# One product with B per unit, later stores of y, and results of the side work taken one step later over three banks

## The chip, the cores and the metric

The kernel runs on one core of one Trainium2 chip. The metric is the device time of one execution in microseconds; the median of several runs is given. The engines are named as the profile names them: PE is TensorE's matmul, PEld its weight load, DVE is VectorE, ACT is ScalarE, POOL is GpSimd, SP is SyncE, which issues the DMAs here.

## The reference

The input `x` is 16 images of 256 channels on 32 x 32 positions (1024 tokens). Two layers are added to it in turn, each on a group-normalised input:

```python
x = x + _L0_conv_ref(_gn(x), ...)   # layer norm, attention of 4 heads, feed-forward of 128
x = x + _L1_conv_ref(_gn(x), ...)   # state-space scan with 512 channels and 64 states
```

The second layer, cut to what matters here:

```python
u, z = jnp.split(xs @ in_proj_w.T, 2, axis=-1)
u = jax.nn.silu(causal_conv(u, conv_w, 4 taps) + conv_b)
dt, Bm, Cm = jnp.split(u @ x_proj_w.T, [DT_RANK, DT_RANK + D_STATE], axis=-1)
delta = jax.nn.softplus(dt @ dt_proj_w.T + dt_proj_b)
def step(h, inp):                       # over 1024 tokens
    d_t, B_t, C_t, u_t = inp
    h = jnp.exp(d_t[..., None] * A) * h + (d_t * u_t)[..., None] * B_t[:, None, :]
    return (h, jnp.einsum('bdn,bn->bd', h, C_t))
y = (ys + u * D) * jax.nn.silu(z)
return (y @ out_proj_w.T) * ctx         # ctx: sigmoid of a convolution over tokens
```

## The kernel before

**The scan.** Its work is cut into 4096 units, 256 for each of the 16 batches: two halves `t` of 512 tokens, four blocks `k` of 128 channels, four quarters `q`, eight units `i`. A unit holds four channels with all their 64 states: 128 partitions are 64 states times two channels, and `e` runs over the two other ones. The main loop (L973) emits for unit n, in this order:

- `load(n + 6)`: SP fetches delta times u for four channels, broadcast over the states, into a tile `dub` of 128 x 2 x 512 (seven buffers). One such load is 512 KB. At the start of a quarter it also fetches `pieces`, at the start of a half the tiles `bt` and `ct`.
- `inputs(n + 4)`: POOL multiplies `dub` in place by `bt` (the B of the reference), in two instructions of 128 x 512 (L869).
- `scan(n, 0)` and `scan(n, 1)`: DVE's scan over 512 tokens (L891). It reads the decays `a` from PSUM and the product from SBUF, and writes `h`.
- `decay(n + 2)`: PE picks the deltas of four channels out of `pieces` into two PSUM banks (L878) and ACT takes the exponential in place (L881). Pool `aps` has four banks, two units' worth; the banks of unit n + 2 are those that unit n's scans have read.
- steps of the side work, as many as are due (below).
- `outputs`: a generator that runs one stretch per unit for each finished quarter. PE multiplies `h` with the spread C (`cd`, L928) in two rounds, ACT copies each round to `y2` (L936), PE turns it (L940), ACT copies the result to `yo` (L948), and one unit later SP stores it in four DMAs (L954). The tile `yb`, one PSUM bank, is taken and half cleared on DVE at the start of each half `t` (L918). `cd`, 128 x 4096, is taken and cleared on POOL once in each batch (L903); `spread_c` fills it with eight activations (L907) in unit 6 of each half.

**The side work** is all that the next batch needs (`first_norm`, `attention_layer`, `scan_inputs`) and what the last one still lacks (`gate_and_store`), written as generators. Each `yield` gives the share of time that the step before it is held to be worth. The loop hands steps out by credit:

```python
if at >= (1 if b + 1 < B else 8):
    due += rate
    while due > 0.0:
        due -= next(side, 1e9)
```

Here `at` is the number of the unit in its batch, and `rate` is the sum of all shares divided by 247, so about one step is emitted in each unit; a small share lets two steps into one unit, a large one leaves a unit without a step. In the last batch only `gate_and_store` is left.

**Order.** The loop at the end (L1022 to L1032) ties each instruction of PE, ACT, DVE and POOL to the one before it on its engine, so every engine runs its instructions in the order in which they were written.

**PSUM.** Eight banks: four for the decays (`aps`), one for `yb`, one (`accp`) for the sums `av` of the attention, two (`mm`) for the side work's results. `psum()` takes its bank from `mm` while the scan runs, and from `mm` and `aps` in turn before and after it.

**Names that are spoken of later.** `group_norm`: mean (PE), subtraction (DVE L249), squares (ACT), variance (PE), reciprocal root (ACT L260, L261), product (DVE L264); it runs twice for a batch. `layer_norm`: the same by halves of 512 tokens (means L272, subtraction L279, reciprocal root L296 and L298, product L303); also twice. In `scan_inputs`, z is PE L607, tanh on ACT L612, product on DVE L596 in `finish_z`; `project` and `tap` are the causal convolution (L628, L633, L634, L642); softplus is `begin` (PE L713, ACT L715, L716), `more` (ACT L721, L722), `rest` (DVE L726, L727) and the logarithm (ACT L739). In `gate_and_store`, `us` and `ys` are joined on DVE (L787, L791), and the last product goes through `m_ps` (PE L816, DVE L803 and L805 in `finish`). L642, L682, L787, L791, L330, L584, L539 and L515 are the DVE instructions that read two tensors in SBUF.

Of the kernel before, what the change touches and what calls it, by code (L numbers as in the profile page):

```python
# [11 lines left out]
F32 = mybir.dt.float32  # L12
BF16 = mybir.dt.bfloat16
AF = mybir.ActivationFunctionType
ALU = mybir.AluOpType
# [4 lines left out]
P = 128  # L20
# [3 lines left out]
HL = 512  # L24
# [9 lines left out]
TB = 512  # L34
# [18 lines left out]
def attention_then_scan_kernel(  # L53
# [18 lines left out]
    nc = tc.nc  # L72
# [13 lines left out]
    hst = pool("hst", 1)  # L86
# [11 lines left out]
    def psum(name, dims=P):  # L98
        src = mm if beside["scan"] else next(alone)
        return src.tile([P, HL], F32, name=name, tag="mm" if src is mm else "a")[:dims]  # L100

    def work(name, n=L):
        return wide.tile([P, L + 2 + CONV], F32, name=name, tag="wide")[:, :n]
# [4 lines left out]
    def hs(h):  # L108
        return ts(h, HL)
# [73 lines left out]
    for k in range(KC):  # L183
# [5 lines left out]
        nc.sync.dma_start(rel[ts(k, P), :], t)  # L189


    def weights(*specs):
# [34 lines left out]
    def group_norm(src, dst):  # L227
# [33 lines left out]
        nc.scalar.activation(v, v, AF.Exp, scale=-0.5)  # L261
        yield 1.5
        for k in range(KC):
# [4 lines left out]
    def layer_norm(src, dst, g, b):  # L268
        def mean_of(parts, name):
            m = psum(name)  # L270
            for k in range(KC):
                nc.tensor.matmul(m, avg, parts[k], start=(k == 0), stop=(k == KC - 1))  # L272
            return m

        def centre(h, m):
            qs = []
            for k in range(KC):
                d = dst[k][:, hs(h)]
                nc.vector.tensor_tensor(d, src[k][:, hs(h)], m, ALU.subtract)  # L279
                q = hwork("ln_sq")  # L280
                nc.scalar.activation(q, d, AF.Square)
                qs.append(q)
            return qs

        m = mean_of([t[:, hs(0)] for t in src], "ln_m")
        yield 1
        q0 = centre(0, m)
        m = mean_of([t[:, hs(1)] for t in src], "ln_m")
        yield 1.2
        q1 = centre(1, m)  # L290
        vs = [mean_of(q0, "ln_v")]
        yield 1.2
        vs.append(mean_of(q1, "ln_v"))
        yield 1
        for v in vs:
            nc.scalar.activation(v, v, AF.Ln, bias=eps)  # L296
        for v in vs:
            nc.scalar.activation(v, v, AF.Exp, scale=-0.5)  # L298
        yield 2
        for h in range(2):  # L300
            for k in range(KC):
                d = dst[k][:, hs(h)]
                nc.vector.tensor_tensor(d, d, vs[h], ALU.mult)  # L303
                nc.scalar.activation(d, d, AF.Identity, bias=col(b, k), scale=col(g, k))
            yield 1.2
# [258 lines left out]
    def scan_inputs(b):  # L564
# [27 lines left out]
        ready = []  # L592

        def finish_z():
            for d, hf, z, t, ps in ready:
                nc.vector.scalar_tensor_tensor(z[:, hs(hf)], t, 1.0, ps, ALU.add, ALU.mult)  # L596
                if hf == 1:
                    nc.sync.dma_start(zs[ts(d, P), :], z)
            ready.clear()

        for d in range(ND):
            z = work("z")
            for hf in range(2):
                finish_z()
                ps = psum("z_ps")
                for k in range(KC):
# [124 lines left out]
        for d in range(ND):  # L731
            items = [more(d, *items[0]), begin(d, 1)]
            yield 1
            items[1] = more(d, *items[1])
            rest(*items[0])
            yield 1.4
            rest(*items[1])
# [32 lines left out]
    def gate_and_store(b):  # L770
# [39 lines left out]
        for o in range(KC):  # L810
            for hf in range(2):
                ps = psum("m_ps")
                for q in range(2):
                    first = o * HL + hf * 2 + q
                    for d in range(ND):
# [3 lines left out]
                        )  # L819
                    if q == 0:  # L820
                        finish()
# [43 lines left out]
    def inputs(n):  # L865
        b, t = units[n][:2]
        for e in range(2):
            v = loaded[n][:, e, :]
            nc.gpsimd.tensor_tensor(v, v, blocks[b, t]["bt"], ALU.mult)  # L869

# [28 lines left out]

    def spread_c(b, t):  # L900
        if t == 0:
            now["cd"] = hst.tile([P, TB // 16, P], F32, name="cd", tag="cd")
            nc.gpsimd.memset(now["cd"], 0.0)  # L903
        ct = blocks[b, t]["ct"].rearrange("p (a c e) -> p a c e", c=4, e=4)
        for c in range(4):
            for j in range(2):
                nc.scalar.activation(  # L907
                    now["cd"][:, :, 40 * c + j : 40 * c + j + 7 : 2], ct[:, :, c],
                    AF.Identity, scale=par[:, j : j + 1],
                )  # L910
# [4 lines left out]
    def outputs(b, t, k, q):  # L915
        if (k, q) == (0, 0):
            now["yb"] = yps.tile([P, HL], F32, name="yb", tag="yb")
            nc.vector.memset(now["yb"][:, 256:], 0.0)  # L918
        cd, yb, hbuf = now["cd"], now["yb"], now["h", q % 2]
        out4 = yb[:, 256:].rearrange("p (j a m e) -> p a e j m", a=2, j=2, e=4)  # L920
# [27 lines left out]
        nc.scalar.copy(yo, yb[:, 256:])  # L948
        yield
        to = state[b]["ys"][ds(k * P + 32 * q, 32), ts(t, TB)].rearrange(  # L950
# [22 lines left out]
    for n, (b, t, k, q, i) in enumerate(units):  # L973
# [32 lines left out]
        if i == 0 and n > 0:  # L1006
            g = outputs(*units[n - 1][:4])
            next(g)
            running.append(g)
        if (k, q, i) == (0, 0, 6):  # L1010
            spread_c(b, t)
    for g in running:
# [75 lines left out]
```

## Time and profile before

| what | value |
|---|---|
| median of 3 runs | 13546.32 us (13542.6 to 13555.92) |
| profiled execution | 13547.65 us, its span 13545.9 us |
| granted TensorE clock, mean | 0.766 |
| DVE, POOL, PE, ACT busy | 12092.7, 10483.0, 10672.8, 7925.4 us |
| before the first scan, from the first to the last scan, after it | 387.7, 13112.7, 45.5 us |
| the two scans of a unit | 1.20 us each for t = 0, 1.26 us for t = 1 |
| product with B on POOL | 1.27 us (median) x8192 |
| DMA | 208 GB/s on average, 61% of the 16 engines' time |

A line of the groups names source line, engine, operation, output and inputs, and count, and after it busy time, mean length of one, and what ended the idle time ahead of it. A line of the waits names who waited for whom, the time in total, the number of times and the longest. A line of the timeline gives the start and the length in us, with the idle time ahead in brackets. "Unit 218" is the unit with that number in its batch.

### The profile page before, as it was taken

The page shows a single profiled execution, that of the slowest core. Times are in us where ns is not written, and L with a number is a line of the kernel's source. Part 1 is how long each engine was busy: PE and PEld are TensorE (multiplying, and loading weights), DVE is VectorE, ACT ScalarE, POOL GpSimd, SP SyncE. Part 2 cuts the span into 40 slices and gives each one's busy share as a digit, 9 for nine tenths or more (in the row PEclk, how much of TensorE's full clock was granted, in tenths as well). Part 3 has the DMA queues.
Part 4 walks back from the last instruction along what each step waited for, and adds up shares of the span by engine and source line. Part 5 has one row for each costly group of instructions (what it writes and reads, how often), then busy time and mean ns, then how long its engine had stood idle before and what let it go on. Part 6 is the DMA issues. An engine that isn't in the chain of part 4 may idle for free. (4 is left out here: it accounts for less than half of the span.)

```text
span 13545.9 us, 437083 instructions
## 1 busy us (share of the span) xinstructions
PE 10672.8 (79%) x186800; PEld 5381.9 (40%) x186800; DVE 12092.7 (89%) x11683; ACT 7925.4 (59%) x13941; POOL 10483.0 (77%) x8214
## 2 busy tenths in 40 slices
PE   7787878878787787877878778787887878878757
PEld 3344344433444334443344434434343343433434
DVE  3899999899998989989898998999988999899898
ACT  3666665656656566655656646566565665656644
POOL 0687878878787787877878778787887877878788
PEclk8786877868688686876868778687786877868767
DMA  1566566665666656656666666656666566665666
GB/s 60 198 208 235 196 215 217 205 229 200 208 217 202 228 200 219 210 202 222 207 230 197 204 219 210 232 195 207 220 204 229 197 215 214 201 231 202 203 218 225
DMA packets 1001958, 2821.36 MB, mean 208 GB/s; under 512 B 175810, under 2 KB 319427, under 8 KB 1000004
## 3 DMA queue, kind: packets, MB, share of 16 engines
q1 hardware_dynamic: 1000004, 2793.39, 61.1%
q8 instruction: 1460, 23.92, 0.7%
q14 instruction: 494, 4.05, 0.1%
HBM read 2514.18 MB, written 261.62 MB: 205 GB/s over the span
## 5 line engine op out<-in xcount | busy, mean ns | idle before, releaser
L869 POOL TENSOR_TENSOR dub<-dub,bt 128x512 f32<-128x512 f32 x8192 | 10428.0, 1307 | 3013.2 <-DMA dub<-dus 2609.3
L881 ACT ACTIVATE a<-a,acol 128x512 f32<-128x512 f32 x8192 | 5070.3, 660 | 3815.8 <-PE a L878 3783.7
L891 DVE TENSOR_TENSOR_SCAN h<-a,last,dub 128x512 f32<-128x512 f32 x4096 | 4928.7, 1261 | 136.2 <-POOL dub L869 76.9
L891 DVE TENSOR_TENSOR_SCAN h<-a,dub 128x512 f32<-128x512 f32 x4096 | 4695.9, 1202 | 287.8 <-POOL dub L869 209.5
L878 PE MATMUL a<-pieces,pick 48*128 48x512 bf16 x8192 | 2967.8, 466 | 2345.9 <-DVE h L891 2265.8
L928 PEld LDWEIGHTS yb<-h,cd 128*32 128x32 f32 x131072 | 2563.5, 135 | 2036.9 <-issue 1671.6
L928 PE MATMUL yb<-h,cd 128*32 128x64 f32 x131072 | 2963.2, 258 | 148.9 <-DVE yb L918 108.3
L878 PEld LDWEIGHTS <-pick 48*128 48x128 bf16 x8192 | 520.9, 96 | 2514.6 <-issue 2312.0
L403 PE MATMUL s_ps<-k,q 32*64 32x512 f32 x4096 | 889.3, 717 | 59.1 <-DVE mx L384 57.9
L940 PEld LDWEIGHTS yb<-turn,y 128*16 128x16 f32 x32768 | 408.8, 119 | 1010.9 <-ACT y L936 473.1
L936 ACT COPY y<-yb 128x256 f32<-128x256 f32 x1024 | 383.7, 375 | 728.9 <-PE yb L928 722.9
L384 DVE TENSOR_REDUCE mx<-s_ps 128x1 f32<-128x512 f32 x1024 | 646.1, 675 | 23.6 <-PE s_ps L403 21.5
L940 PE MATMUL yb<-turn,y 128*16 128x32 f32 x32768 | 538.9, 212 | 107.0 <-ACT y L936 97.2
L471 PE MATMUL st_ps<-sp 33*128 33x512 f32 x2048 | 601.1, 632 | 16.7 <-ACT pt L479 15.0
L459 PE MATMUL av<-pt,vv 128*64 128x512 f32 x2048 | 582.7, 648 | 5.6 <-ACT sums L448 3.3
L479 ACT ACTIVATE pt<-st_ps 128x512 f32<-128x512 f32 x1024 | 557.4, 605 | 48.7 <-PE st_ps L471 47.1
L657 PE MATMUL g_ps<-w,xp 128*128 128x256 f32 x1536 | 447.4, 446 | 0.0
L403 PEld LDWEIGHTS s_ps<-k,q 32*64 32x64 f32 x4096 | 207.0, 148 | 580.3 <-DVE mx L384 541.5
L657 PEld LDWEIGHTS g_ps<-w,xp 128*128 128x128 f32 x1536 | 388.9, 328 | 98.6 <-issue 75.0
L816 PE MATMUL m_ps<-w,xs 128*128 128x256 f32 x1024 | 310.5, 452 | 12.0 <-DVE xs L791 12.0
L642 DVE SCALAR_TENSOR_TENSOR u<-up,cwh,u 128x1024 f32<-128x1024 f32 x192 | 285.0, 1485 | 31.8 <-ACT u L634 31.5
L816 PEld LDWEIGHTS m_ps<-w,xs 128*128 128x128 f32 x1024 | 258.8, 328 | 89.8 <-issue 61.4
(135 smaller groups left out, 7122.9 us busy)
## 6 DMA issues: line engine op xcount, KB each, us to landing
dub<-dus SPq DMA_DIRECT2D x4096, 512.0 KB
dps<-pc SPq DMA_DIRECT2D x384, 128.0 KB
pieces<-dps SPq DMA_DIRECT2D x1024, 48.0 KB
xs<-in_x_dram SPq DMA_DIRECT2D x64, 512.0 KB
xs<-kept SPq DMA_DIRECT2D x64, 512.0 KB
zs<-z SPq DMA_DIRECT2D x64, 512.0 KB
ud<-u SPq DMA_DIRECT2D x64, 512.0 KB
dus<-du SPq DMA_DIRECT2D x64, 512.0 KB
```

The costliest lines, as they stand in the source:

```text
L384: nc.vector.tensor_reduce(mx[:, g, c, hf : hf + 1], s, AX.X, ALU.max)
L403: nc.tensor.matmul(waiting[g][0][ts(e, 64)], q4[r, ts(c, 64)], k4[r, hs(hf)], start=True, stop=True,)
L459: nc.tensor.matmul(av[ts(e, 2 * DH)], vv[j // (NJ // 2)][:, j % (NJ // 2), 2 * pair + e, :], pts[e], start=(j == 0), stop=(j == NJ - 1),)
L471: nc.tensor.matmul(s, ka[r, ts(j, P)], qa[r, hs(hf)], start=True, stop=True)
L657: nc.tensor.matmul(ps[:, ts(q, C)], xp[k][:, ds(first + t, P, 4)], wg_s[:, k, t, :], start=(i == 0), stop=False,)
L816: nc.tensor.matmul(ps[:, ts(q, C)], us[d][:, ds(first, P, 4)], wo_s[:, d, :], start=(d == 0), stop=(d == ND - 1),)
L869: nc.gpsimd.tensor_tensor(v, v, blocks[b, t]["bt"], ALU.mult)
L878: nc.tensor.matmul(a, w, pieces[r], start=True, stop=True)
L881: nc.scalar.activation(a, a, AF.Exp, scale=acol[:, at : at + 1])
L891: nc.vector.tensor_tensor_scan(now["h", q % 2][:, 2 * i + e, :], decays[n][e], loaded[n][:, e, :], first, ALU.mult, ALU.add,)
L928: nc.tensor.matmul(yb[ts(g, 32), ts(s, 64)], cd[:, at // 16, ts(c, 32)], hbuf[:, :, at : at + 4], start=(c == 0), stop=(c == 3),)
L940: nc.tensor.matmul(out4[32 * s : 32 * s + 16, half, e], y2[:, 64 * s + e : 64 * s + 64 : 4], turn[:, e], start=True, stop=True,)
```

## The change

- `inputs` issues one POOL instruction of 128 x 2 x 512, with `bt` broadcast over the two, in place of two instructions.
- `cd` and `yb` are taken and cleared once before the scan, no longer once in each batch and in each half. `spread_c` does half of its eight activations in unit 5 and half in unit 6.
- After the copy to `yo`, `outputs` lets three stretches pass in place of one before SP stores it.
- `psum3` hands out the two banks of `mm` and the one of `accp` in turn; the means and variances of `layer_norm`, z and `m_ps` use it.
- `group_norm` and `layer_norm` have a step without work between reciprocal root and product; `layer_norm` issues both means in two steps ahead of the first subtraction.
- `finish_z` keeps the newest result for the next step, and `finish` in `gate_and_store` is called after the second half of the next product.
- Softplus: `more` of half 0, then `begin` of half 1 with `rest` of half 0, then `more` of half 1, then `rest` of half 1.

```diff
+    three = cycle((mm, mm, accp))
+
+    def psum3(name):
+        src = next(three) if beside["scan"] else next(alone)
+        return src.tile([P, HL], F32, name=name, tag={mm: "mm", accp: "av"}.get(src, "a"))
...
+    cd = hst.tile([P, TB // 16, P], F32, name="cd", tag="cd")
+    nc.gpsimd.memset(cd, 0.0)
+
+    yb = yps.tile([P, HL], F32, name="yb", tag="yb")
+    nc.vector.memset(yb, 0.0)
...
         nc.scalar.activation(v, v, AF.Exp, scale=-0.5)
-        yield 1.5
+        yield 1.2
+        yield 1
         for k in range(KC):
             nc.vector.tensor_tensor(grouped(dst[k]), grouped(dst[k]), over_group(v), ALU.mult)
...
         def mean_of(parts, name):
-            m = psum(name)
+            m = psum3(name)
...
-        m = mean_of([t[:, hs(0)] for t in src], "ln_m")
-        yield 1
-        q0 = centre(0, m)
-        m = mean_of([t[:, hs(1)] for t in src], "ln_m")
+        m0 = mean_of([t[:, hs(0)] for t in src], "ln_m")
+        yield 0.7
+        m1 = mean_of([t[:, hs(1)] for t in src], "ln_m")
+        yield 0.7
+        q0 = centre(0, m0)
         yield 1.2
-        q1 = centre(1, m)
         vs = [mean_of(q0, "ln_v")]
+        q1 = centre(1, m1)
         yield 1.2
         vs.append(mean_of(q1, "ln_v"))
-        yield 1
+        yield 0.8
...
             nc.scalar.activation(v, v, AF.Exp, scale=-0.5)
-        yield 2
+        yield 1.3
+        yield 1
...
-        def finish_z():
-            for d, hf, z, t, ps in ready:
+        def finish_z(keep=0):
+            while len(ready) > keep:
+                d, hf, z, t, ps = ready.pop(0)
                 nc.vector.scalar_tensor_tensor(z[:, hs(hf)], t, 1.0, ps, ALU.add, ALU.mult)
                 if hf == 1:
                     nc.sync.dma_start(zs[ts(d, P), :], z)
-            ready.clear()
...
-                finish_z()
-                ps = psum("z_ps")
+                finish_z(1)
+                ps = psum3("z_ps")
...
         for d in range(ND):
-            items = [more(d, *items[0]), begin(d, 1)]
-            yield 1
+            items[0] = more(d, *items[0])
+            yield 0.8
+            items.append(begin(d, 1))
+            rest(*items[0])
+            yield 1.3
             items[1] = more(d, *items[1])
-            rest(*items[0])
-            yield 1.4
+            yield 0.8
             rest(*items[1])
...
-                ps = psum("m_ps")
+                ps = psum3("m_ps")
...
-                    if q == 0:
+                    if q == 1:
                         finish()
...
         b, t = units[n][:2]
-        for e in range(2):
-            v = loaded[n][:, e, :]
-            nc.gpsimd.tensor_tensor(v, v, blocks[b, t]["bt"], ALU.mult)
+        v, bt = loaded[n], blocks[b, t]["bt"]
+        nc.gpsimd.tensor_tensor(v, v, bt.unsqueeze(1).to_broadcast([P, 2, TB]), ALU.mult)
...
-    def spread_c(b, t):
-        if t == 0:
-            now["cd"] = hst.tile([P, TB // 16, P], F32, name="cd", tag="cd")
-            nc.gpsimd.memset(now["cd"], 0.0)
+    def spread_c(b, t, some):
...
-        if (k, q) == (0, 0):
-            now["yb"] = yps.tile([P, HL], F32, name="yb", tag="yb")
-            nc.vector.memset(now["yb"][:, 256:], 0.0)
-        cd, yb, hbuf = now["cd"], now["yb"], now["h", q % 2]
+        hbuf = now["h", q % 2]
...
         nc.scalar.copy(yo, yb[:, 256:])
-        yield
+        for _ in range(3):
+            yield
...
-        if (k, q, i) == (0, 0, 6):
-            spread_c(b, t)
+        if (k, q) == (0, 0) and i in (5, 6):
+            spread_c(b, t, ((0, 1), (2, 3))[i - 5])
```

More of the change, by code (lines that the diff above doesn't have):

```diff
@@ L896, in scan @@
             del decays[n], loaded[n]
-    def spread_c(b, t):
-        if t == 0:
-            now["cd"] = hst.tile([P, TB // 16, P], F32, name="cd", tag="cd")
-            nc.gpsimd.memset(now["cd"], 0.0)
+    def spread_c(b, t, some):
         ct = blocks[b, t]["ct"].rearrange("p (a c e) -> p a c e", c=4, e=4)
-        for c in range(4):
+        for c in some:
             for j in range(2):
                 nc.scalar.activation(
-                    now["cd"][:, :, 40 * c + j : 40 * c + j + 7 : 2], ct[:, :, c],
+                    cd[:, :, 40 * c + j : 40 * c + j + 7 : 2], ct[:, :, c],
                     AF.Identity, scale=par[:, j : j + 1],
```

## The prediction

> **What bounds the kernel now.** I read the engine shares first, then VectorE's waits, then the timeline around the longest kinds of wait.
>
> ```profile
> PE 10672.8 (79%) x186800; PEld 5381.9 (40%) x186800; DVE 12092.7 (89%) x11683; ACT 7925.4 (59%) x13941; POOL 10483.0 (77%) x8214
> ```
>
> VectorE (DVE) is the tightest engine. By the stage view it is busy 11926 of the 13113 us between the first and the last scan, so at most 1187 us of idle can be won there. DVE's waits, longest in total first (us in total, times, longest):
>
> ```profile
> DVE h L891 <- POOL dub L869: 286.3, 234, 9.9
> DVE d_ps L726 <- ACT d_ps L722: 148.7, 90, 22.6
> ...
> DVE xn L303 <- ACT ln_v L298: 105.1, 32, 5.1
> DVE z L596 <- ACT z_t L612: 96.4, 69, 3.0
> DVE gn L264 <- ACT gn_v_ps L261: 96.2, 16, 7.9
> DVE m_ps L803 <- PE m_ps L816: 91.6, 60, 4.7
> ```
>
> The first line misleads: in the trace the product has ended 9.1 us (median) before its scan starts, so most of these waits are for ScalarE's `a`, held up in ScalarE's queue. The others are results of the side work, asked for too early. How early is too early shows in unit 218 of a middle batch (start us, length us) on DVE:
>
> ```profile
> 5225.38 3.61 DVE L891 TENSOR_TENSOR_SCAN h<-a,last,dub 128x512 f32<-128x512 f32 x3
> 5233.05 0.70 DVE L726 SCALAR_TENSOR_TENSOR d_ps<-sp_s,d_ps 128x512 f32<-128x512 f32 x1 [4.06 <-ACT d_ps L722]
> ```
>
> and ScalarE:
>
> ```profile
> 5230.69 1.24 ACT L881 ACTIVATE a<-a,acol 128x512 f32<-128x512 f32 x2 [0.17 <-PE a L878]
> 5231.84 0.63 ACT L721 ACTIVATE sp_s<-sp_e 128x512 f32<-128x512 f32 x1
> 5232.36 0.66 ACT L722 ACTIVATE d_ps<-d_ps,vec 128x512 f32<-128x512 f32 x1
> ```
>
> Here `more` and `rest` of one half fall into the same unit. ScalarE must first do the decays of two units ahead, whose PSUM banks only this unit's scans free: scans end at 5228.99, TensorE's picks, two exponentials (1.24), then L721 and L722 (1.18), and DVE waits 4.06. Without TensorE's y work ahead of the picks (1.9 us) the floor is picks to first exponential 0.68, 1.15 to L721, 1.18: 3.0 us. **A result of ScalarE used in the unit that issues it costs 3.0 to 4.1 us, used one unit later 0 to 1.7** (the same line at 5264.09 waits 1.65, the next half 0).
>
> What two operands in SBUF cost (ns min/median/max):
>
> ```profile
> L642 DVE SCALAR_TENSOR_TENSOR u<-up,cwh,u x192: 1250/1274/2374, 282.5 to 12642.2; 128x1024 f32<-128x1024 f32 x192
> ```
>
> beside an instruction of the same size with one input in PSUM:
>
> ```profile
> L249 DVE TENSOR_TENSOR gn<-xs,gn_m_ps x32: 1193/1218/1222, 26.0 to 12010.3; 128x1024 f32<-128x1024 f32 x32
> ```
>
> and an extreme from the last batch, on DVE's timeline:
>
> ```profile
> 13083.96 15.01 DVE L787 SCALAR_TENSOR_TENSOR xs<-xs,vec 128x1024 f32<-128x1024 f32 x1
> ```
>
> **What the Trainium skill says.** "SBUF — State Buffer", Who interferes with whom: a VectorE instruction with two SBUF inputs contends with a GpSimd instruction that reads SBUF, and the port pair is held for the whole instruction. The trace agrees: L249, with one input in PSUM, never exceeds 1.22 us; L642 reaches 2.37, its excess being what remained of the product in flight; L787 sat 15 us behind back-to-back products. "GPSIMD Engine Reference", 3.1: a 2048-element product takes 4497 ns. With this trace's 1.27 us for 512, a straight line gives an estimate of 2.35 us for 1024, against 2 x 1.22 (spacing in back-to-back stretches) = 2.44. "PSUM — Partial Sum Buffer", Engine vs sequencer instructions: ScalarE's, VectorE's and GpSimd's queues are strict FIFO, which is why a side result waits behind the decays; the timeline above agrees.
>
> **The change, part by part.** The sum is against the profiled execution: span 13545.9, with what lies around it 13547.65; the median of the runs is 13546.32, 1.3 lower. I added up the yields by the loop's rule (each unit credits `rate`, steps run while credit lasts) and compared with the order of instructions on DVE and ScalarE in both programs. The shares of a middle batch go from 274.4 to 278.8, `rate` from 1.111 to 1.129, so every later step shifts. Batches 1 to 14 have one plan; batch 0 runs at 1.003 and 1.021 and I set its changes to nothing (its waits are short on both sides); batch 15 has only the gate.
>
> Gains, per batch and then x14:
> - First group norm: reciprocal root in unit 7, product moved from unit 8 to 9; its wait is 6 to 7.9. The memset of `cd` on POOL, for which ScalarE waited 62.5/15 = 4.2, is gone. 6.3 x14 = 88.
> - Second group norm: product two units after instead of one; its 2.7 goes: 38.
> - First layer norm: unit 42 instead of 41; 4.0 falls to about the 2.4 that the second one has with two units between: 28, with a little for the evenly issued means. The second keeps its two units (146 to 148, now 145 to 147): nothing.
> - z: half 21 no longer finishes in the unit of its tanh (2.5), the others (0.4) wait no more; the first keeps 2.7, TensorE being late. 2.9 x14 = 41.
> - m_ps: the first three of each gate (3.7, 0.5, 0.4) get another unit, the last not: 64.
> - Two qk products in unit 44 and two v in unit 81 are pulled apart; the decays they delay cost 3.2 and 2.4. But the last qk now shares a unit with the first score product, which waits for it: I keep 20 of 78.
> - Memsets of `yb` (8.7 us) and second layer-norm means: 15. TensorE's 108 us of waiting for that memset lie beside DVE's own wait in unit 8: nothing more.
> - POOL: 4096 x 0.09 = 370 us less, hidden by the lead of four units; only the last batch (675 us for 256 units, POOL 2.44 each) is near POOL's pace: 25, bounds 0 and 50.
> Together 319.
>
> The stores of y move two steps later, past two loads of `dub`. SP waits 557.6 us for `yo` in L954, but products lie 9 us ahead: nothing, and up to 20 if that lead is gone.
>
> Losses:
> - Softplus. Shares 0.8 and 1.3 are no longer a unit each: `more` and `rest` of half 0 share units 208, 217, 226 and 235 (before only 218), of half 1 units 219, 228 and 237 (before none). Seven waits at 3.7 plus 0.5 are 26.4, less the 7.9 of now, less 3.3 of waits for a late `a` in units 208 and 209 that fall inside the first: 15.2 x14 = 213. Bounds 140 (floor 3.0) and 290 (4.06, nothing absorbed). Behind the waiting DVE instruction stand the next scans, and behind those the freed banks, the picks and ScalarE.
> - First tap in the unit (178) of its own projection: 1.7 becomes about 3.7 (picks, 1.3 of matmul, 1.4 of ScalarE): 28.
> - The port. 512 DVE instructions read two SBUF tensors; their excess over the undisturbed length sums to 198 us, 57 of it from four starved L787. About 150 of the 512 start during a unit's first product and now meet the second in the same instruction: 150 x 1.1 = 165; fewer where phases shift, so 150. Bounds: 0 (they come at ends of products, as half do now) and 280 (uniform arrival: 72% x 1.08 x 512 = 400, less what there is).
> - `ud` fetched one unit later before the gate, the first scan waiting for the whole product (slack under 2.2 us in 2% of units): 15, bounds 0 and 45.
> Together 406. Net +87: **13,633 us** on the median's basis.
>
> 0.2% is about what a measurement of this kernel can tell from no change: 27 us.
>
> **Rivals.**
> - *The port isn't held longer where it matters*: faster. DVE's two-input instructions keep meeting the last stretch of a product. The port then costs 0 to 36, the point below which all is faster than 13,520; at zero 13,483, with the softplus at its floor 13,410. For: the median of L642 is only 20 ns over its minimum. Against: the excess equals the remainder in all blocked cases, and a third start in first products.
> - *Full price*: uniform arrival and unabsorbed waits: 280 + 290 + 43 - 270 (layer norm and pulled-apart products giving nothing) = +343, 13,890. For: the wait of 4.06 recurs in nearly every batch. Against: TensorE is ahead after a stall.
> - *A tie*: gains and losses within 27, 13,546; TensorE, 90% busy in the z and tap stages, gives both signs away.
> - *It doesn't do what it says*: for softplus, second layer norm and last m_ps the result is not taken later; this is already in the main case.
>
> **Chances.** Main case 0.42, full price 0.14 (both slower), tie 0.11, faster 0.33. The main case's own range is 13,580 to 13,720; for 8 in 10 it reaches to 13,400 and 13,850.
>
> **What would show it.** Right: the waits on the two group norms, z and m_ps nearly gone; the softplus wait near 380 us instead of 149, with waits of 3 to 4 us in units 217, 219, 226 and 228; a product of about 2.35 us x4096; L642's counterpart with a mean above 1.75 us (now 1.485); scans unchanged at 1.20 and 1.26. Wrong: softplus waits under 200, or taps at their old length, or new waits for POOL's product. If the scans themselves change length, the whole sum is off.
>
> PREDICTION {"us": 13633.0, "low": 13400.0, "high": 13850.0, "faster": 0.33, "same": 0.11, "slower": 0.56}

## The result and the profile after

The changed kernel takes 13684.5 us, median of 4 runs (13667.04 to 13707.92), against 13544.46 us (13525.22 to 13555.92) for the kernel before beside it: a ratio of 1.0104, 95% interval 1.0091 to 1.0117. It is slower by 140 us. Its profiled execution took 13670.78 us, 123 more than the profiled execution of before. The forecast was 13,633 and slower.

The line numbers of the changed kernel differ: the scan is L908 (before L891), the product L886 (L869), softplus L731 to L743 (L715 to L727), the first tap's line L658 (L642), the group norm's product L278 (L264), the pick L895 (L878), the exponential L898 (L881).

Engine shares of the changed kernel:

```profile
PE 10775.1 (79%) x186800; PEld 5459.9 (40%) x186800; DVE 12151.0 (89%) x11652; ACT 7915.3 (58%) x13941; POOL 9708.2 (71%) x4103
```

POOL works 775 us less (724 of it by the product, where the forecast had 370), and this buys almost nothing: VectorE (DVE) is the engine that counts, its busy time is 58 us up, and its idle time (span less busy) goes from 1453 to 1518 us. DVE's waits show which idle time (total, times, longest):

```profile
DVE d_ps L742 <- ACT d_ps L738: 381.7, 128, 22.6
DVE h L908 <- issue: 360.8, 329, 4.2
DVE h L908 <- POOL dub L886: 162.2, 109, 3.9
DVE few L519 <- DMA few<-den: 136.4, 16, 96.4
DVE xn L319 <- ACT ln_v L313: 77.8, 32, 5.1
DVE u L658 <- ACT u L650: 59.2, 16, 4.0
...
DVE z L613 <- ACT z_t L628: 40.8, 24, 3.1
...
DVE m_ps L821 <- PE m_ps L834: 36.4, 18, 4.7
...
DVE gn L278 <- ACT gn_v_ps L274: 10.4, 16, 2.5
DVE xp L278 <- ACT gn_v_ps L274: 8.2, 16, 3.8
```

Against the list of before: softplus (first row) is up by 233 us. The two group norms (`gn` and `xp`, before 96.2 and 42.2), z, m_ps and the layer norm are down by 259 together. The scans' waits stand in two rows under different names, in the list of before as

```profile
DVE h L891 <- POOL dub L869: 286.3, 234, 9.9
DVE h L891 <- issue: 132.6, 210, 3.7
```

so take them from the trace as one: 424 us before, 530 after.

The product and the tap by their lines (ns min/median/max):

```profile
L886 POOL TENSOR_TENSOR dub<-dub,bt x4096: 2327/2353/3433, 350.2 to 13612.7; 128x1024 f32<-128x1024 f32 x196
```

```profile
L658 DVE SCALAR_TENSOR_TENSOR u<-up,cwh,u x192: 1249/1526/3328, 272.6 to 12784.0; 128x1024 f32<-128x1024 f32 x192
```

The tap's minimum is the same; median and maximum have grown with the product.

Softplus in a middle batch. On DVE, units 217 to 219:

```profile
5266.85 4.79 DVE L908 TENSOR_TENSOR_SCAN h<-a,last,dub 128x512 f32<-128x512 f32 x4
5274.77 0.70 DVE L742 SCALAR_TENSOR_TENSOR d_ps<-sp_s,d_ps 128x512 f32<-128x512 f32 x1 [3.13 <-ACT d_ps L738]
...
5276.11 4.80 DVE L908 TENSOR_TENSOR_SCAN h<-a,last,dub 128x512 f32<-128x512 f32 x4
5283.95 0.70 DVE L742 SCALAR_TENSOR_TENSOR d_ps<-sp_s,d_ps 128x512 f32<-128x512 f32 x1 [3.04 <-ACT d_ps L738]
```

and on ScalarE (ACT) for the first of them:

```profile
5272.41 1.24 ACT L898 ACTIVATE a<-a,acol 128x512 f32<-128x512 f32 x2 [1.20 <-PE a L895]
5273.56 0.63 ACT L737 ACTIVATE sp_s<-sp_e 128x512 f32<-128x512 f32 x1
5274.08 0.66 ACT L738 ACTIVATE d_ps<-d_ps,vec 128x512 f32<-128x512 f32 x1
```

DVE's last scan ends at 5271.64. Only then are its banks free for the picks. ACT takes the two exponentials, then L737 and L738, and DVE stands idle for 3.13 us until its operand is there.

The length of a batch, counted between first scans: batches 1 to 14 go from 831.1 to 841.5 on average, batch 0 from 801.0 to 824.5, batch 15 from 675.7 to 640.6.

In what follows, two sums stand beside the times. **Port excess**: for each of the 512 DVE instructions that read two tensors in SBUF, its length less the undisturbed length of its shape (1.20 us, 1.25 for L642 and L787, 0.68 for L515, lines of the kernel before), summed over those with less than 5 us of it. **Starved**: the same sum over those with more. Before they are 140 and 58 us, after 253 and 30.

### The profile page after: what moved, and what is told of

Same layout as the page of the kernel before. It is cut to its first block, busy times and chain, and to the rows that moved or that the text cites. A ratio compares the mean times of both kernels' runs of the same rounds, so it can differ in the third digit from the quotient of the medians.

```text
span 13669.0 us, 429258 instructions
## 1 busy us (share of the span) xinstructions
PE 10775.1 (79%) x186800; PEld 5459.9 (40%) x186800; DVE 12151.0 (89%) x11652; ACT 7915.3 (58%) x13941; POOL 9708.2 (71%) x4103
## 5 line engine op out<-in xcount | busy, mean ns | idle before, releaser
L886 POOL TENSOR_TENSOR dub<-dub,bt 128x1024 f32<-128x1024 f32 x4096 | 9704.0, 2385 | 3906.2 <-DMA dub<-dus 3351.9
L898 ACT ACTIVATE a<-a,acol 128x512 f32<-128x512 f32 x8192 | 5081.0, 661 | 3937.1 <-PE a L895 3913.1
L908 DVE TENSOR_TENSOR_SCAN h<-a,last,dub 128x512 f32<-128x512 f32 x4096 | 4925.3, 1260 | 144.4 <-issue 118.5
L908 DVE TENSOR_TENSOR_SCAN h<-a,dub 128x512 f32<-128x512 f32 x4096 | 4689.8, 1199 | 385.7 <-issue 242.3
L895 PE MATMUL a<-pieces,pick 48*128 48x512 bf16 x8192 | 2947.9, 467 | 2404.6 <-DVE h L908 2325.4
L939 PEld LDWEIGHTS yb<-h,cd 128*32 128x32 f32 x131072 | 2614.1, 137 | 1939.0 <-issue 1693.5
L939 PE MATMUL yb<-h,cd 128*32 128x64 f32 x131072 | 3012.2, 261 | 16.9 <-issue 12.7
L895 PEld LDWEIGHTS <-pick 48*128 48x128 bf16 x8192 | 514.3, 96 | 2687.2 <-issue 2488.7
L487 PE MATMUL st_ps<-sp 33*128 33x512 f32 x2048 | 646.8, 642 | 24.1 <-ACT pt L495 22.7
L742 DVE SCALAR_TENSOR_TENSOR d_ps<-sp_s,d_ps 128x512 f32<-128x512 f32 x128 | 89.1, 696 | 381.7 <-ACT d_ps L738 381.7
L658 DVE SCALAR_TENSOR_TENSOR u<-up,cwh,u 128x1024 f32<-128x1024 f32 x192 | 327.8, 1708 | 59.5 <-ACT u L650 59.2
```

The lines of the kernel that those rows point to most:

```text
L487: nc.tensor.matmul(s, ka[r, ts(j, P)], qa[r, hs(hf)], start=True, stop=True)
L886: nc.gpsimd.tensor_tensor(v, v, bt.unsqueeze(1).to_broadcast([P, 2, TB]), ALU.mult)
L895: nc.tensor.matmul(a, w, pieces[r], start=True, stop=True)
L898: nc.scalar.activation(a, a, AF.Exp, scale=acol[:, at : at + 1])
L908: nc.vector.tensor_tensor_scan(now["h", q % 2][:, 2 * i + e, :], decays[n][e], loaded[n][:, e, :], first, ALU.mult, ALU.add,)
L939: nc.tensor.matmul(yb[ts(g, 32), ts(s, 64)], cd[:, at // 16, ts(c, 32)], hbuf[:, :, at : at + 4], start=(c == 0), stop=(c == 3),)
```

## The experiments

All times are medians with the ratio to the kernel before on the same chip and its 95% interval.

### e1: one product, nothing else

```diff
-        for e in range(2):
-            v = loaded[n][:, e, :]
-            nc.gpsimd.tensor_tensor(v, v, blocks[b, t]["bt"], ALU.mult)
+        v, bt = loaded[n], blocks[b, t]["bt"]
+        nc.gpsimd.tensor_tensor(v, v, bt.unsqueeze(1).to_broadcast([P, 2, TB]), ALU.mult)
```

> The kernel before with the one product of 128 x 2 x 512 per unit, and nothing else of the change; the plan of the side work stays as it was. Theory 'two costs' (the longer product holds the SBUF port longer against DVE's two-input instructions): L642's mean goes from 1.485 to about 1.7 us, DVE's busy time rises by 90 to 150 us, time 13,620 to 13,680; the scans' waits stay near 419 us. Rival 'the product is a gain, something else costs': L642 stays at 1.5 us and the time is 13,500 to 13,550. Rival 'late products': the scans' waits for POOL grow by some 100 us, L642 unchanged.

Measured: 13608.2 us, ratio 1.0043 (1.0028 to 1.0058), so 57 us slower, 12 us short of the range of 'two costs'. Port excess goes from 140 to 260, starved from 58 to 32, the scans' waits stay (424 and 425), and the last batch is 23 us shorter. The line of the tap in e1:

```profile
L642 DVE SCALAR_TENSOR_TENSOR u<-up,cwh,u x192: 1249/1382/3435, 283.4 to 12710.3; 128x1024 f32<-128x1024 f32 x192
```

What follows: the longer product alone is a loss, by the port. Part of it is repaid in the last batch, where the starved instructions of before stand (see e12).

### e2: softplus with wider shares

The changed kernel with `more` and `rest` of one half a unit apart; the last line stands for the four steps that follow in the same loop. The total of the shares is the same, so all steps before softplus keep their units.

```diff
             items[0] = more(d, *items[0])
-            yield 0.8
+            yield 1.2
             items.append(begin(d, 1))
             rest(*items[0])
             yield 1.3
             items[1] = more(d, *items[1])
-            yield 0.8
+            yield 1.2
             rest(*items[1])
...
-            yield 1.4
+            yield 1.2
```

> The changed kernel with softplus in its new order, but shares of 1.2, 1.3, 1.2, 1.7 and four times 1.2 (before the edit 0.8, 1.3, 0.8, 1.7 and four times 1.4; the sum is the same, so every step outside softplus stays in its unit). By the loop's rule no `rest` is in the unit of its `more` any more. Theory 'two costs': the wait of L742 falls from 382 us to 100 to 160, and the time by about as much, to 13,405 to 13,465. Rival 'the stall only moves' (TensorE and ScalarE are behind anyway): L742's wait falls but the scans' waits grow by nearly as much; time 13,620 to 13,700.

Measured: 13466.65 us, ratio 0.9940 (0.9925 to 0.9955): 218 us faster than the changed kernel, and faster than before. The softplus row in the waits of e2:

```profile
DVE d_ps L742 <- ACT d_ps L738: 145.8, 128, 22.6
```

What follows: 236 us of wait taken away give 218 us of time. The whole loss of the change, and more, hangs on the shares of one loop.

### e3 and e4: two products again, in the changed kernel and in e2

The diff is that of e1, backwards.

> The changed kernel with the two products of 128 x 512 per unit put back, all else and the plan as changed. Theory 'two costs': L658's mean goes from 1.708 to about 1.5 us, the time falls by 90 to 140 to 13,545 to 13,595, and the scans' waits stay near 520 us, since the plan makes them. Rival 'late products': the scans' waits fall back to about 420 us. Rival 'the product is a gain': slower than 13,684 by 20 to 60.

Measured: 13673.99 us, ratio 1.0096 (1.0079 to 1.0113): 10 us faster than the changed kernel, which is less than the interval, and not 90 to 140. Port excess falls from 253 to 139 us, but starved rises from 30 to 81 and the last batch from 641 to 675 us. Scan waits stay at 550.

> Both edits: softplus's steps apart and two products per unit, all else as changed. Theory 'two costs' with costs that add: 13,684 less about 250 and about 115, so 13,290 to 13,350, faster than both kernels. If the costs share the same time (a stall in one place gives TensorE and ScalarE a lead that saves the next), the sum is less than the parts: 13,380 to 13,450. Rival 'the stall only moves': above 13,550.

Measured: 13461.68 us, ratio 0.9937 (0.9922 to 0.9952), about the same as e2; the first expectation missed by over 100 us, the second (costs that share the same time) by 12. Again the last batch is longer (692 us against 639) and starved higher (95 against 24).

What follows: in the changed plan the long product costs in one place nearly what it brings in another. And the scans' new waits are not the product's: they are there with two products too.

### e5: the new softplus order, in the kernel before

```diff
-            items = [more(d, *items[0]), begin(d, 1)]
-            yield 1
+            items[0] = more(d, *items[0])
+            yield 0.7
+            items.append(begin(d, 1))
+            rest(*items[0])
+            yield 1.0
             items[1] = more(d, *items[1])
-            rest(*items[0])
-            yield 1.4
+            yield 0.7
             rest(*items[1])
```

> The kernel before with the new order of the softplus steps alone, with shares 0.7, 1.0, 0.7 so that the total and every step up to unit 205 stay as they were; `more` and `rest` of one half then share a unit four times in batches 1 to 14 (halves 0 and 1 of the first and third group or their neighbours), instead of once. Theory (each such coincidence costs 3.7 us on VectorE plus about 0.5): waits of d_ps on ScalarE rise from 149 us to about 290, the time by 90 to 150 us, ratio 1.007 to 1.011. Rival (the stall is absorbed behind TensorE or gives it a lead that is won back at the late decays): the waits rise, the time by less than 30 us.

Measured: 13681.16 us, ratio 1.0086 (1.0070 to 1.0102), 115 us slower. By the trace the four shared units of a batch (209, 218, 228, 237) wait 2.85, 3.88, 3.04 and 3.05 us; all softplus waits rise from 149 to 279. What follows: the coincidence costs its wait in the other plan as well, and little is absorbed, 130 us of wait for 115 of time.

### e6: four products of 256

```diff
         for e in range(2):
-            v = loaded[n][:, e, :]
-            nc.gpsimd.tensor_tensor(v, v, blocks[b, t]["bt"], ALU.mult)
+            for p in range(2):
+                v = loaded[n][:, e, ts(p, TB // 2)]
+                nc.gpsimd.tensor_tensor(v, v, blocks[b, t]["bt"][:, ts(p, TB // 2)], ALU.mult)
```

> The kernel before with four products of 128x256 for each unit in place of two of 128x512. Theory (a DVE instruction with two SBUF inputs waits for the rest of the product in flight, so its excess goes with the product's length): product about 0.7 us, mean of the tap line L642 from 1.485 to about 1.36 us, two-input excess from 140 to about 80 us; GpSimd's busy time rises by 400 to 600 us. Rival (what counts is GpSimd's share of the port over time, not the length of one instruction): excess unchanged or higher.

Measured, in one run: 13854.83 us, 299 more than the kernel before beside it. The product, and two of the lines with two inputs in SBUF (the groups' view: busy, mean ns, idle before):

```profile
L870 POOL TENSOR_TENSOR dub<-dub,bt 128x256 f32<-128x256 f32 x16384 | 11670.7, 757 | 2079.2 <-DMA dub<-dus 1822.7
```

```profile
L642 DVE SCALAR_TENSOR_TENSOR u<-up,cwh,u 128x1024 f32<-128x1024 f32 x192 | 306.0, 1594 | 32.1 <-ACT u L634 31.8
...
L515 DVE TENSOR_TENSOR ao<-ao,sums 128x512 f32<-128x512 f32 x32 | 168.7, 5276 | 56.7 <-DMA sums<-den 56.7
```

I expected the tap at 1.36 us and got 1.594; POOL's busy time rose by 1243 us in place of 400 to 600. Counting for each of the 512 instructions how many products it waited through shows two effects:

| kernel | product | waited through one product, mean wait | waited through 5 or more |
|---|---|---|---|
| e6 | 0.73 us | 321, 0.18 us | 22, in all 262 us |
| before | 1.27 us | 396, 0.30 us | 4, in all 58 us |
| changed | 2.35 us | 365, 0.69 us | 2, in all 23 us |

The wait for one product does go with its length, 24 to 29% of it. But with more and shorter products POOL runs longer stretches back to back, and then a DVE instruction can be passed over again and again: 13 of the 32 L515 stand behind 12 to 21 products (mean of the line 5.28 us, its undisturbed length 0.68), an L787 behind 27. So the theory held for the wait for one product, and the rival for the sum: port excess 118 and starved 262 are 380 us, before 198.

### e7: later stores of y, nothing else

```diff
         nc.scalar.copy(yo, yb[:, 256:])
-        yield
+        for _ in range(3):
+            yield
```

> The kernel before with the stores of y two steps later, nothing else. Theory (products lie 12 us ahead of their scans, so what SP issues when does not matter): within 0.2% of before, waits of the scans unchanged at about 424 us. Rival (the stores, now behind later loads, hold back loads of dub or collide with them): scans start with less than 2 us of slack in more than 2% of the units, and the time rises by 20 us or more.

Measured: 13526.76 us, ratio 0.9970 (0.9961 to 0.9978), 39 us *faster*. The expectation missed; neither case was right. Two waits tell why, SP's for `yo` and DVE's for the attention's sums, before

```profile
SPq L954 <- ACT yo L948: 557.6, 282, 12.0
...
DVE ao L515 <- DMA sums<-den: 56.4, 15, 5.5
```

and in e7:

```profile
SPq L955 <- ACT yo L948: 62.8, 43, 12.2
...
DVE ao L515 <- DMA sums<-den: 11.6, 11, 5.8
```

SP's queue in the kernel before, in a batch in which `ao` waits:

```profile
4101.68 1.71 SPq L954 DMA_DIRECT2D ys<-yo  x4
4103.43 0.52 SPq L859 DMA_DIRECT2D dub<-dus  x1
4104.82 0.34 SPq L505 DMA_DIRECT2D den<-few  x1
4107.10 2.87 SPq L859 DMA_DIRECT2D dub<-dus  x2
4110.06 1.93 SPq L508 DMA_DIRECT2D sums<-den  x4
```

and in e7, the same place:

```profile
4084.68 0.34 SPq L505 DMA_DIRECT2D den<-few  x1
4085.08 0.89 SPq L955 DMA_DIRECT2D ys<-yo  x2
4086.96 0.52 SPq L859 DMA_DIRECT2D dub<-dus  x1
4087.58 1.93 SPq L508 DMA_DIRECT2D sums<-den  x4
```

The `sums` go out 2.9 us behind `den` in place of 5.2, with one load of `dub` between instead of two, and `ao`'s wait at this point falls from 2.80 to 0.23 us. What follows: the stores were not in the way of the products, which I had looked at, but of the small transfers of the side work in the same queue. DVE's idle time falls by 39 us, `ao`'s share of it by 45.

### e8: `cd` and `yb` cleared once, spread_c in two parts

```diff
+    cd = hst.tile([P, TB // 16, P], F32, name="cd", tag="cd")
+    nc.gpsimd.memset(cd, 0.0)
+    yb = yps.tile([P, HL], F32, name="yb", tag="yb")
+    nc.vector.memset(yb, 0.0)
...
-        if (k, q, i) == (0, 0, 6):
-            spread_c(b, t)
+        if (k, q) == (0, 0) and i in (5, 6):
+            spread_c(b, t, ((0, 1), (2, 3))[i - 5])
```

> The kernel before with `cd` and `yb` taken and cleared once ahead of the scan, and with spread_c split over units 5 and 6; nothing else. Theory: the wait of the first group norm's product falls from 138 us in all (both group norms) to about 75, the 31 short memsets of yb on VectorE go (9 us); time 50 to 80 us less, ratio 0.994 to 0.9965. Rival (the wait passes to the next in line, the two tok additions or the next scans' decays): the wait falls but the time by less than 30 us.

Measured: 13519.82 us, ratio 0.9962 (0.9945 to 0.9980), 46 us faster. The first group norm's wait, 96.2 us before, is in e8:

```profile
DVE gn L271 <- ACT gn_v_ps L268: 41.4, 16, 2.7
```

What follows: most of it is real, 55 us of wait for 46 of time, a little under the 50 to 80 that I expected; the gate's wait for `ud` is 30 us higher in this run.

### e9: one product in the last batch alone, on e2

```diff
         v, bt = loaded[n], blocks[b, t]["bt"]
-        nc.gpsimd.tensor_tensor(v, v, bt.unsqueeze(1).to_broadcast([P, 2, TB]), ALU.mult)
+        if b + 1 < B:
+            for e in range(2):
+                nc.gpsimd.tensor_tensor(v[:, e, :], v[:, e, :], bt, ALU.mult)
+        else:
+            nc.gpsimd.tensor_tensor(v, v, bt.unsqueeze(1).to_broadcast([P, 2, TB]), ALU.mult)
```

> The changed kernel with the softplus shares of e2 and two products per unit in batches 0 to 14, one product in batch 15 alone. Theory (the port price of the longer product falls on the side work of batches 0 to 14, its saving of GpSimd time counts only in the last batch): batches 1 to 14 as in e4 (825.4 us), batch 15 as in e2 (639 us instead of 692): 40 to 60 us below e4 in the profiled span, about 13,410 to 13,430. Rival (the length of the last batch has nothing to do with GpSimd's pace, but with where its few gate steps meet the products): batch 15 stays above 670 and the time within 0.2% of e2 and e4.

Measured: 13429.86 us, ratio 0.9904 (0.9886 to 0.9921). Batches 1 to 14 take 824.7 us as in e4, batch 15 takes 637.6 as in e2. What follows: this is why e3 and e4 moved so little. One product costs about 0.36% (49 us, e2 against e9) in batches 0 to 14 and saves about 0.33% (45 us, e4 against e9) in batch 15, each to about 0.23% either way. The traces have 37 and 54 us for the two; 16 of the 54 are e4's own, whose last batch is 17 us longer than that of e3 with the same two products in it.

### e10: the remaining coincidences pulled apart, on e9

The places in their order in the code: q and k, v, the sums of the attention (twice), the empty steps behind them (twice), the relative position, z.

```diff
-                yield 1
+                yield 1.13
...
-            yield 1
+            yield 0.9
...
-                yield 1
+                yield 1.1
...
-        yield 0.8
+        yield 0.4
...
-            yield 1.4
+            yield 1.1
...
-                yield 1
+                yield 1.05
```

> e9 with other shares for the projections of q and k (1.13), v (0.9), the sums of the attention (1.1), the two empty steps behind them (0.4), the relative-position additions (1.1) and z (1.05). The total stays within 0.1, the attention's 36 steps fall into the same units as in the kernel before, the last qk projection and the first scores no longer share a unit, nor do the last projection of u and the first tap. Theory (a late `a` comes from score steps that meet TensorE's y rounds; shares alone decide it): waits of scans in units 80 to 132 fall from about 20 to about 15 us per batch, the first-tap wait from 59 to about 32 us, time 60 to 110 us below e9, about 13,320 to 13,370. Rival (the late `a` belongs to the stage, whose TensorE and ScalarE are full, and only changes its unit): scan waits stay near 560 us, the time within 30 us of e9.

Measured: 13357.18 us, ratio 0.9848 (0.9828 to 0.9868), 73 us below e9. Scan waits in units 80 to 132 are 15.5 us a batch; they were 15.4 before, 20.7 in the changed kernel, 21.4 in e9. The tap waits 41 us instead of 59, f2 (the addition behind the feed-forward, L570) 3.5 instead of 33, z 15 instead of 38; `ao` gives 32 back. What follows: where the score steps fall decides whether decays come late. The tap keeps more than the 32 us that I expected. Yet this is the fastest version here, 1.5% below the kernel before and about 2.5% below the changed one.

### e11: the side work's new steps alone

> The kernel before with the side work's new steps alone: three banks, group norm, layer norm, z, m_ps, and softplus in the new order but with the shares of e2 that keep `more` and `rest` of one half apart; two products per unit, y stores, `cd` and `yb` as before. Theory (what these steps save in waits, about 200 us, comes back almost whole as late decays in other units, first tap, scores and f2): e4 without the parts measured in e7 (-39) and e8 (-46), so within 0.3% of before, 13,520 to 13,580; scan waits near 550 us, waits of z, m_ps and layer norm as in e4. Rival (the parts do not add: the steps are worth their saved waits and e7's and e8's gains vanish in their presence): 13,440 to 13,490.

Its edit is that of e4 without the parts of e7 and e8. Measured: 13519.87 us, ratio 0.9962 (0.9950 to 0.9974), 43 us faster, between the two expectations and at the edge of the first. Waits of group norms, layer norm products, z and m_ps are 256 us lower than before, `ao` 48 and the layer norm means 31 lower; those of scans are 171 higher, the gate's for `ud` 43, tap 28, `few` (reciprocals of the attention's sums) and mx (maxima of its scores) 19 each, f2 11. That is 335 against 291, and the idle time falls by 60. What follows: more than four fifths of the waits won at these places come back at others (15 of the 19 us of `few` are one wait ahead of the scan, which the steps need not have made).

### e12: one product in the last batch alone, on the kernel before

Its edit is that of e9. 

> The kernel before with one product in batch 15 alone. Theory (the last batch, with little side work, runs near GpSimd's pace): batch 15 falls from 676 to about 645 us and the rest stays, time 20 to 40 us less, ratio 0.997 to 0.9985. Rival (the last batch is not set by GpSimd): batch 15 stays within 10 us and the time within 15 us.

Measured: 13538.31 us, ratio 0.9978 (0.9967 to 0.9988), 24 us faster; batch 15 falls from 676 to 655 us.

What follows: the product's length counts in the last batch, but not as POOL's pace. Only eight DVE instructions there read two tensors in SBUF, the gate's L787 and L791. They are longer than undisturbed by 59 us in all before and by 39 in e12, which is the whole gain; in the changed kernel by 35, in e4 by 81 and in e9 by 30. The scans of that batch take 625 to 628 us in each of these, and DVE is idle for 14 us of it before and 15 in e12.

## Why the prediction was right, and where not

The sign and the main cause were right; the sum was 52 us short on the medians (87 forecast, 140 measured). Behind it stand hits and four misses that partly cancel, so that the sum came out as near as this is in part luck.

**Softplus, forecast 213 in batches 1 to 14: hit.** The trace gives for these batches, unit by unit, 2.88, 0.69, 3.12, 3.04, 3.94, 3.13, 3.04 and 3.12 us, together 22.96 against 7.73 before: 15.2 more, times 14 is 213. Seven shared units were forecast and seven came, in units 208, 217, 219, 226, 228, 235 and 237. That it is 213 to the microsecond is luck, as two sizes were off and cancel. The seven waits at 3.7 and 0.5 more were to make 26.4 us a batch; their mean is 3.2. And 3.3 was to come back in the scans' waits of units 208 and 209 (1.73 and 1.52 before); only the 1.5 of unit 209 went, and it goes in e2 too, where no long wait of softplus could take it in. e2 shows that the wait is time (218 us) and e5 that it isn't a matter of this plan.

**Batch 0, forecast nothing: wrong.** Its softplus waits rise by 20.5 us, nearly all of its 23.5. "its waits are short on both sides" was read from before; at a share of 0.8 the steps fall together there too.

**Group norms 126, layer norm 28, z 41, m_ps 64: right as waits, wrong as time.** They sum to 259, and these waits fell by 259 in the profile (120, 27, 57, 55; that the sums agree so well is chance). But a saved wait counts only if DVE isn't held up at the next place. The step that failed is the last of the gains, "I keep 20 of 78": apart from this and the 3.3 us absorbed under softplus I took the scans' waits for late decays as given. They rose by 106. The second group norm, layer norm, z and m_ps alone stood in the sum with 171; e11, which has these, the first group norm's new step and the first tap's loss, measured 43.

Unit 30 shows one form of it: its scan never waited before, now 2.4 us on average in batches 1 to 14, behind the m_ps steps which no longer hold DVE up. The larger form is in the attention: units 99, 110 and 123 wait 3.3, 2.9 and 3.3 us on average, before 0.0, 0.2 and 1.1. DVE in unit 98 and 99 of a middle batch:

```profile
4881.66 3.44 DVE L908 TENSOR_TENSOR_SCAN h<-a,dub 128x512 f32<-128x512 f32 x3
4888.89 1.22 DVE L908 TENSOR_TENSOR_SCAN h<-a,dub 128x512 f32<-128x512 f32 x1 [3.79 <-POOL dub L886]
```

The releaser named is POOL, but products end 13 us (median of all units; 12.2 before) ahead of their scans in this kernel. TensorE's line tells the real one:

```profile
4881.69 2.56 PE L487 MATMUL st_ps<-sp 33*128 33x512 f32 x4
4884.18 1.98 PE L475 MATMUL av<-pt,vv 128*64 128x512 f32 x4
4886.08 1.67 PE L939 MATMUL yb<-h,cd 128*32 128x64 f32 x64
4887.69 0.39 PE L895 MATMUL a<-pieces,pick 48*128 48x512 bf16 x2
```

The pick for unit 99 stands behind 6 us of scores, values and y work, and the exponential follows at 4888.14. By the sum of the shares, and by the order of instructions on ACT, three score steps of this stretch now fall into units 94, 95 and 96, where the third had fallen into 97: the changed `rate`, 1.129 for 1.111, and the parted v moved them. I had written that every later step shifts, and then priced only the shifts that I had looked for. e3 clears the product of this; e10 shows the cause, since with the steps put back into their old units by shares alone the three waits are 0.0, 0.3 and 0.7 us.

**Port, forecast 150, bounds 0 and 280: right in kind, too large.** Port excess rose by 113, and 28 of starved went: net 85, of which 109 more in batches 0 to 14 and 24 less in the last one. e1, with the gain of the last batch inside, gives 57 us of time; with that gain from e12 taken off, 81 for batches 0 to 14, and in the changed plan 49 (e2 against e9). The term mis-sized is the 150 instructions that meet the second half of a product at 1.1 each: the mean wait for one product rose from 0.30 to 0.69 us, and 31 instructions fewer wait. The tap's mean is 1.708, a little under the 1.75 forecast. The product's length is 2.353 us; the estimate of 2.35 took this trace's 1.27 and the figure of the Trainium skill ("GPSIMD Engine Reference", 3.1), which is that of an addition of two tensors.

**Last batch, forecast 25, bounds 0 and 50: the number hit, by luck.** It is 24 in e12, about 45 in e9, 35 in the profile of after. But the term was reckoned as POOL's pace, and what fell is the port's hold on eight DVE instructions (59 to 39 us in e12, 59 to 35 after). The prediction had counted 57 of these 59 us under the port, and as unchanged. Another 10 of the 35 are scans' waits in that batch, which fall in e8 as well, where `cd` isn't cleared again. Why the eight are held for less with the long product isn't shown.

**Stores of y, forecast nothing, up to 20 of loss: wrong, a gain of 39.** Failed step: "products lie 9 us ahead: nothing". It asks only about one of the queue's customers. SP's wait for `yo` also holds `sums`, and DVE's 56.4 us for `ao` stood in the list of before.

**`cd` and `yb`.** Forecast as part of the first group norm and 15 for memsets and means; e8 gives 46 us by itself.

**`ud`, forecast 15:** its wait rose by 22. **First tap, forecast 28:** its wait rose by 28. **Scans** kept 1.20 and 1.26 us.

The runs do not add exactly: e7, e8 and e11 make 128 together, e4, which holds all three, is 85 to 90 below before. With softplus at 218 and the product at about 5 to 10, that gives 133 to 138, which is what the change costs. The overlap of 40 is little more than the intervals of the four runs together allow (37), and why it is there is open; e11 has `ao` at 8 us with the stores unmoved, so part of e7's gain is in its plan already.

One rival to all of this was not tested: the granted clock goes with the time. It is 0.761 to 0.764 in the changed kernel's four runs and 0.765 to 0.766 on average in each of the four sets of runs of the kernel before that stand beside the experiments; within these sets a clock lower by 0.001 goes with 4 to 7 us more. Whether that is a cause or an effect isn't shown; as a cause it would make some 20 of the 140 us (an estimate from these figures), and as much of the 73 between e9 (0.770) and e10 (0.773).

Of the rivals, the port at 0 to 36 is excluded by e1 for the plan of before; over the whole program of after it is what is left (10) once the last batch is set against it. Full price fails on the port, and a tie within 27 on the 140. That softplus would not be taken later was true, and was the case itself.

## What to carry to other kernels

A step "one later" is one later only if its share is at least the rate at which steps are issued; work out which steps fall into the same unit before and after, and price each coincidence by the wait that the trace already shows for one. A change of any share moves all later steps, so look at where the heavy stages land, not only at those that were edited. And when a wait of a DMA queue goes, ask for everything that is queued behind it, the small transfers of the side work first. A part that hits its number can still have another path: look which instructions got shorter.

## What the runs showed of the hardware

- A DVE instruction with two SBUF inputs that meets a product on POOL gets through about 0.12 us before the product's end as reckoned from its undisturbed length, so it waits for all of the rest: 0.18, 0.30 and 0.69 us on average for products of 0.73, 1.27 and 2.35 us.
- It does not always get the next turn. Behind products without a gap between them, single instructions stood for 5 to 27 products, up to 17.6 us: 22 times in e6 with four products a unit, 4 times in the kernel before with two, twice in the changed one with one; e3 and e4, with two in the changed plan, have 8 and 9. In the kernel before and in the changed one all of these were released only when POOL paused for over 7 us, and so were nine in e6; thirteen there got through at the end of one product like the others. What lets one through and not another was not found out. The Trainium skill ("SBUF — State Buffer", Who interferes with whom) gives the port pair to one side for the whole of an instruction; the 0.12 us above agrees with that.
- In one case followed in the trace, the pause comes of the wait itself. POOL's line beside the L787 of 13083.96, which lasts until 13098.97:

```profile
13081.97 15.91 POOL L869 TENSOR_TENSOR dub<-dub,bt 128x512 f32<-128x512 f32 x13
```

  After that POOL has no loaded tile left. SP issues the next load at 13101.24, behind scans that stand behind L787, and POOL goes on at 13105.25. So this wait ended when the loaded tiles were used up. With seven `dub` these are at most 7, 14 and 28 products with one, two and four a unit, and no wait counted is longer: 7 at most with one (e2), 14 with two (e3), 27 with four (e6).
- A product of 1024 elements takes 2.353 us (median), one of 512 takes 1.27, one of 256 takes 0.727: four of these are 0.37 us more than two.
- An operand from ScalarE used in the unit that issues it made DVE wait 2.9 to 3.9 us (means of batches 1 to 14, the changed kernel's softplus), used a unit later 0.5 to 1.7 (e2).
